# Where GpSimd's record scatters stand in layer 0 of a graph network: in one run ahead of the row gathers, or in four parts between later stages

## The chip, the cores and the metric

The kernel runs on one core of a Trainium2 chip. The metric is the device time of one execution in microseconds; a time "of the kernel" is the median of several executions. Profiled executions are single ones and have a time of their own.

## The reference, cut to what matters

Four layers work on 3125 nodes of 256 features and on 53125 edges (50000 random ones and a loop at every node). Each layer adds a sum over edges and a mixer over nodes, and then a mixture of experts:

```
x = x + _L0_gnn_ref(xn, src, dst, edge_weight, ...) + _L0_mix_ref(xn[None], ...)[0]
x = x + _L0_ffn_ref(_layernorm(x, axis=-1)[None], ...)[0]
```

In layer 0, `_L0_gnn_ref` is `h = xn @ W.T + b`, then `segment_sum(edge_weight * h[dst], src)` and an ELU. `_L0_mix_ref` is linear attention over all nodes (sums of keys times values come first, then each node's query is applied to them), a layer norm, a two-layer network of width 1024 and another layer norm. `_L0_ffn_ref` sends each node through one shared hidden layer of width 1024 and one of eight output layers, the one with the greatest gate. Layers 1 to 3 use other graph sums and mixers; what matters here is that layer 0 sums over edges in order of their source, and that layer 1 (and 2) need the edges in order of their destination.

## The kernel before, in words

**Nodes.** The 3125 nodes stand as 25 tiles of 128 rows, the 25 tiles of x stay in on-chip memory. A "pair" below is two such tiles: the mixer and its two-layer network work on 12 pairs and a single last tile.

**Edges are sorted on the chip.** The class `Sorted` computes for each of the 53125 edges (416 columns of 128) its place in a list that is ordered by one key and padded so that each of 440 blocks ("slots") of 128 edges belongs to one node tile. `put_records` (L193) then moves the edges there: 416 indirect DMAs, issued one after the other by GpSimd, each of which writes 128 records of 16 bytes to scattered rows of a DRAM table. This is done twice: `rec_src` (ordered by source, for layer 0's sum) and `rec_dst` (ordered by destination, for layers 1 and 2). `read` (L358) loads a finished table back, and `tiles_as_columns` (L205, L206) transposes it on TensorE into columns of keys, indices and weights that later instructions use. The two sets of places are computed by `places` (L270 to L282); the second set is put away in DRAM by `leave` and fetched again by `take` (the loads of `posi` and `r` from `kept_dst`), because the space is needed in between.

**Layer 0's graph sum.** `project` (L422) writes h to DRAM. `weighted_sums` goes over the 440 slots: `gather` (L503), an indirect DMA issued by GpSimd, fetches the 128 rows of h that the slot's edges name, VectorE builds a selection matrix (L540), TensorE multiplies the two (`aggp`, L542), and VectorE adds the product to the slot's node tile in `acc` (L544). Six tiles `g` take turns as targets of the gathers.

**The mixer is interleaved by a generator.** `mix0` is a generator of 140 steps. The caller takes `ahead` of them before the graph sum (1000 before the change, which means all of them), and the sum takes one step after every second slot while there are steps left. Its normalising step transposes node tiles (`pt`, L460, copied by ScalarE at L462); then come keys and values (`kvp`), and for each pair queries, attention, the two-layer network (`hp`, `fp`, all through L422, with ScalarE's activation at L1048) and `y` (L1054).

**Who decides the order.** The kernel is written in a tile framework: a scheduler puts each engine's instructions into one order from the program's order, the dependences and its own estimate of when things are ready, and a pool's tile is handed out again when its last reader is done. The engines run their own lists in order and wait for one another by semaphores. GpSimd's list is what this change is about. Before the change it reads: the iota `itile` (L275) of the first sort, 416 `rec_src`, `itile` of the second sort, the zeroing of `acc`, then 416 `rec_dst` mixed with the first 79 gathers, the other gathers, 25 row scatters `f0xs`, 25 row gathers `yrow`, then layer 1's gathers `gk`.

**The expert stage.** `ffn0` normalises x, computes the hidden layer and the gate for 7 groups of up to 4 tiles ("the dense part" below), and the places of the nodes in order of expert; `put_rows` (L1424) scatters the 25 node tiles to `f0xs` in DRAM; `all_biases` (L1318 to L1323) adds the gated bias for 25 tiles; then 8 groups of 4 tiles are loaded back (`x4`, L1557), transposed, sent through the hidden layer and their expert (`yp`, L1568) and stored to `f0ys` (L1571); `take_rows` (L1450) gathers the results into node order (`yrow`). `list_by_dst` reads the `rec_dst` table back, transposes it and stores three rows of it for layer 1.

Of the kernel before, what the change touches and what calls it, by code (L numbers as in the profile page):

```python
# [26 lines left out]
ET = 416  # L27
# [4 lines left out]
NB = NT + 1  # L32
SL = 440
BIG = 1e30
GROUPS = [list(range(t, min(t + 4, NT))) for t in range(0, NT, 4)]
PAIRS = [list(range(t, min(t + 2, NT))) for t in range(0, NT, 2)]

# [66 lines left out]
def edges(c):  # L104

    nc, cp = c.nc, c.const

    c.part = cp.tile([P, 1], F32, name="part")
    nc.gpsimd.iota(c.part, pattern=[[0, 1]], base=0, channel_multiplier=1, allow_small_or_imprecise_dtypes=True)
    c.iota = cp.tile([P, P], F32, name="iota")  # L110
    nc.gpsimd.iota(c.iota, pattern=[[1, P]], base=0, channel_multiplier=0, allow_small_or_imprecise_dtypes=True)
    in_order(c)
    c.by_src = Sorted(c, "src", c.w, ("dst", "edge_weight"), (0, 0))
    c.weights = cp.tile([P, SL], F32, name="weights")
    c.by_src.scatter()
    c.by_dst = Sorted(c, "dst", c.ordered, ("src", "edge_type_64", "dst"), (NP, 0, -1))
    c.by_dst.leave()


# [66 lines left out]
    return v.rearrange("p t -> (p t)").rearrange("(r q e) -> r q e", q=4, e=P)  # L186


def put_records(c, rec, r, at, name):

    nc, tc = c.nc, c.tc
    for t in range(ET):
        i = nc.gpsimd.indirect_dma_start(out=rec, in_=r[:, t, :], in_offset=None,  # L193
                                         out_offset=bass.IndirectOffsetOnAxis(ap=at[:, t:t + 1], axis=0))
        if t:
            tc.declare_no_dep(i.ins, group=f"places {name}", reason="their rows are apart")
        tc.add_to_no_dep_group(f"places {name}", i.ins)


def tiles_as_columns(c, wp, pp, src, dst, n):  # L200

    d = dst.rearrange("p (r q) -> p r q", q=4)
    for q in range(4):
        ps = pp.tile([P, n], F32, name="tcp", tag="tcp")
        c.nc.tensor.transpose(ps, src[:, q, :], c.ident[:n, :n])  # L205
        c.nc.vector.tensor_copy(d[:, :, q], ps)  # L206


def places(c, wp, pp, blk, name, nb=NB):
# [78 lines left out]
class Sorted:  # L288
# [58 lines left out]
        nc.sync.dma_start(self.r.rearrange("p t d -> p (t d)"), self.kept[:, :4 * ET])  # L347
        nc.sync.dma_start(self.at.bitcast(F32), self.kept[:, 4 * ET:])

    def scatter(self):  # L350
        put_records(self.c, self.rec, self.r, self.at, self.key)

    def read(self, more=None):


        c, m = self.c, SL // 4
        b = self.rp.tile([m, 4, P, 4], F32, name="back", tag="r")
        c.nc.sync.dma_start(b, self.rec[:SL * P].rearrange("(r q e) d -> r q e d", q=4, e=P))  # L358
        with c.tc.tile_pool(name="bkp", bufs=2, space=PSUM) as pp:
            for k, d in enumerate((self.k, self.i, more)):  # L360
                if d is not None:
                    tiles_as_columns(c, None, pp, b[:, :, :, k], d, m)
        return b

    def close(self):
# [3 lines left out]
def list_by_dst(c):  # L369

    nc, s = c.nc, c.by_dst
    s.scatter()
    b = s.read()
    c.keys, c.types = (c.dram.tile([SL * P], F32, name=k) for k in ("keys", "types"))
    c.ends = c.dram.tile([SL * P + 2], F32, name="ends")
    nc.sync.dma_start(c.ends[:1], c.low[:1, 0])
    nc.sync.dma_start(c.ends[SL * P + 1:], c.low[:1, 0])
    for j, d in ((0, c.keys), (2, c.types), (3, c.ends[1:SL * P + 1])):
        k = s.rp.tile([SL // 4, 4, P], F32, name=f"row{j}")
        nc.vector.tensor_copy(k, b[:, :, :, j])  # L380
        nc.sync.dma_start(d.rearrange("(r q e) -> r q e", q=4, e=P), k)
    s.close()
# [117 lines left out]


def gather(c, dst, table, idx, t):
    c.nc.gpsimd.indirect_dma_start(out=dst, out_offset=None, in_=table,  # L503
                                   in_offset=bass.IndirectOffsetOnAxis(ap=idx[:, t:t + 1], axis=0))


def nodes(table, t0, n):
# [19 lines left out]
def weighted_sums(c, wp, pp, table, beside):  # L527

    nc = c.nc
    s = c.by_src  # L530
    acc = wp.tile([P, NT, D], F32, name="acc", bufs=1)
    nc.gpsimd.memset(acc, 0.0)  # L532
    for t0 in range(0, SL, 8):
        at = blocks_at(c, s, t0, mybir.EngineType.DVE)
        for j in range(8):
            t = t0 + j
            g = wp.tile([P, D], F32, name="g", bufs=6)
            gather(c, g, table, s.i, t)
            sel = wp.tile([P, P], F32, name="sel", bufs=4)
            nc.vector.tensor_scalar(sel, c.iota, s.k[:, t:t + 1], c.weights[:, t:t + 1], op0=ALU.is_equal, op1=ALU.mult)  # L540
            ps = pp.tile([P, D], F32, name="aggp", tag="agg")
            nc.tensor.matmul(ps, sel, g, start=True, stop=True)  # L542
            a = acc[:, bass.ds(at[j], 1), :]
            nc.vector.tensor_add(a, a, ps[:, None, :])  # L544
            if t % 2:
                next(beside, None)
    for _ in beside:
        pass
    return acc


def gnn0(c, wp, pp, xT, beside, ahead):
    nc = c.nc
    table = c.dram.tile([NROW, D], F32, name="h0")
    project(c, wp, pp, xT, load(c, wp, "L0_gnn_W"), table, load_rows(c, wp, "L0_gnn_b"), bufs=1)
    for _ in zip(beside, range(ahead)):
        pass
    acc = weighted_sums(c, wp, pp, table, beside)

    def finish():  # L560
        for t0 in range(0, NT, 5):
            a = acc[:, t0:t0 + 5, :]
            m = wp.tile([P, 5, D], F32, name="elu", tag="proj", bufs=1)
            nc.vector.tensor_scalar_min(m, a, 0.0)
            nc.scalar.activation(m, m, AF.Exp)
            nc.vector.scalar_tensor_tensor(a, a, 0.0, m, op0=ALU.max, op1=ALU.add)
            xs = c.x[:, t0:t0 + 5, :]
            nc.vector.scalar_tensor_tensor(xs, a, -1.0, xs, op0=ALU.add, op1=ALU.add)

    return finish  # L570


def gnn3(c, wp, pp, xT, beside, ahead):
    table = c.dram.tile([NROW, D], F32, name="h3")
    project(c, wp, pp, xT, load(c, wp, "L3_gnn_weight"), table)
    for _ in zip(beside, range(ahead)):
        pass
    acc = weighted_sums(c, wp, pp, table, beside)

    def finish():  # L580
        for t0 in range(0, NT, 5):
            xs = c.x[:, t0:t0 + 5, :]
            c.nc.vector.scalar_tensor_tensor(xs, acc[:, t0:t0 + 5, :], 0.0, xs, op0=ALU.max, op1=ALU.add)

    return finish
# [834 lines left out]
def put_rows(c, table, places, rows, name):  # L1420

    for pl in places:
        for t in range(NT):
            i = c.nc.gpsimd.indirect_dma_start(out=table, out_offset=bass.IndirectOffsetOnAxis(ap=pl[:, t:t + 1], axis=0),  # L1424
                                               in_=rows[:, t, :], in_offset=None)
            c.tc.declare_no_dep(i.ins, group=name, reason="their rows are apart")
            c.tc.add_to_no_dep_group(name, i.ins)


def experts_of(c, te, t0, n, engines):  # L1430
# [11 lines left out]
def take_rows(c, wp, table, places, weights):  # L1442

    nc = c.nc
    for t in range(NT):
        for pl, w in zip(places, weights):
            y = wp.tile([P, D], F32, name="yrow", bufs=6)
            gather(c, y, table, pl, t)
            x = c.x[:, t, :]
            nc.vector.scalar_tensor_tensor(x, y, w[:, t:t + 1], x, op0=ALU.mult, op1=ALU.add)  # L1450

# [63 lines left out]
def ffn0(c):  # L1515
# [3 lines left out]
    n = 32  # L1519
    with ExitStack() as s:  # L1520
# [11 lines left out]
        with tc.tile_pool(name="f0a", bufs=2) as xa, tc.tile_pool(name="f0ap", bufs=2, space=PSUM) as pp:  # L1532
            xn = xa.tile([P, NT, D], F32, name="xn", bufs=1)
# [13 lines left out]
            pm = largest(c, wp, p, NT, "pm")  # L1547
            co = first(c, wp, p, pm, NT, "co")
            places, te = token_tiles(c, wp, [co], n)
            put_rows(c, xs, places, xn, "f0")  # L1550
            nc.vector.tensor_mul(co, co, p)
            all_biases(c, wp, pp, co, bd)
        lp = s.enter_context(tc.tile_pool(name="f0l", bufs=2))
# [1 line left out]
        for t0 in range(0, n, 4):  # L1555
# [13 lines left out]
                                     start=f == 0, stop=f == 7)  # L1569
                nc.vector.tensor_copy(y4[:, j, :], ps[:, 0, :])  # L1570
            nc.sync.dma_start(nodes(ys, t0, 4), y4)  # L1571
        take_rows(c, lp, ys, places, [pm])


def ffn1(c):
# [122 lines left out]
def mixed(c, i):  # L1698

    tc = c.tc  # L1700
    with ExitStack() as s:
        lp = s.enter_context(tc.tile_pool(name=f"l{i}", bufs=1))
        xT = lp.tile([P, 2, NP], F32, name="xT")
        norm = normalise(c, xT, mp=lp)
        if i == 0:
            c.by_src.read(c.weights)
        gp = s.enter_context(tc.tile_pool(name=f"g{i}", bufs=2))
        gpp = s.enter_context(tc.tile_pool(name=f"g{i}p", bufs=3 if i == 1 else 2, space=PSUM))
        sums = (gnn0, gnn1, gnn2, gnn3)[i]
# [9 lines left out]
        mpp = s.enter_context(tc.tile_pool(name=f"m{i}p", bufs=2, space=PSUM))  # L1719

        beside = (mix0, mix1, mix2, mix3)[i](c, mp, mpp, xT, norm)
        finish = sums(c, gp, gpp, xT, beside, (1000, 8, 8, 8)[i])
        if finish:
            finish()
        if i == 0:
# [3 lines left out]
@with_exitstack  # L1729
def tile_net(ctx, tc, w, out):  # L1730
    c = Net(ctx, tc, w)
    load_x(c)
    constants(c)
    edges(c)
    for i, experts in enumerate((ffn0, ffn1, ffn2, ffn3)):
        mixed(c, i)
        if i == 0:
            c.by_dst.take()
        experts(c)
        if i == 0:  # L1740
            list_by_dst(c)
    store_x(c, out)
# [65 lines left out]
```

## Time and profile before

| | |
|---|---|
| time, median of 3 runs | 8027.63 us (8026.4 to 8031.22) |
| the profiled execution's own time | 8002.89 us |
| its span, first to last instruction | 8001.1 us |
| its mean granted TensorE clock | 0.718 |
| busy share of the span: TensorE, VectorE, ScalarE, GpSimd | 63%, 41%, 12%, 41% |
| `rec_src` scatters on GpSimd | 416, about 114 to 669 us of the span |
| `rec_dst` scatters on GpSimd | 416, 740.0 to 1478.9 us |
| layer 0's gathers on GpSimd | 440, 920.1 to 2161.6 us |
| `f0xs` row scatters, `yrow` row gathers | 25 and 25, from 2384.5 and from 2676.6 us |

The profile is one execution. Its page gives the busy time of each engine and groups of instructions by line; the trace behind it gives each instruction with its start, duration and the time its engine sat idle before it, with the event that ended that idle time ("remote" and "issue" mean that none of the recorded events fits). Times along the span are in microseconds from its start. The profiled execution is 24.7 us, or 0.31%, shorter than the median of the timed runs.

### The profile page before, as it was taken

What the parts mean: (1) busy time and instruction counts of PE and PEld (TensorE: products, weight loads), DVE (VectorE), ACT (ScalarE), POOL (GpSimd) and SP (SyncE); (2) the same over time, 40 slices, a digit from 0 to 9 for tenths busy, and PEclk for the clock granted to TensorE, in tenths of its full rate; (3) what the DMA queues carried; (4) which work ended last, traced back from release to release, by engine and by line L of the source; (5) the groups of instructions that cost most, each with busy time, mean ns of one, the idle gap of its engine ahead of it and who ended that gap; (6) DMA issues with size and microseconds to landing.
All of it is one profiled execution on the core that took longest, in us unless ns stands there. A gap on an engine that the chain in (4) does not pass through costs nothing. (4 is left out here: it accounts for less than half of the span.)

```text
span 8001.1 us, 59679 instructions
## 1 busy us (share of the span) xinstructions
PE 5059.4 (63%) x16612; PEld 3257.6 (41%) x16612; DVE 3313.0 (41%) x8158; ACT 966.9 (12%) x2062; POOL 3283.8 (41%) x3301
## 2 busy tenths in 40 slices
PE   5102323577599776775655795765555998877755
PEld 1001212354265455553333453543433555555334
DVE  3002211354510357766557335544444112545443
ACT  0000001221022111100000011100001223222011
POOL 3775665545500155555762204334341000444632
PEclk6556656787678876666666697865557999988558
DMA  5000100122311244442333113222222000212333
GB/s 170 3 2 20 24 17 16 43 62 75 80 51 43 75 120 128 131 133 75 91 90 86 70 52 108 76 77 78 76 75 60 0 0 30 70 56 62 92 88 110
DMA packets 290607, 542.97 MB, mean 68 GB/s; under 512 B 79731, under 2 KB 170801, under 8 KB 288221
## 3 DMA queue, kind: packets, MB, share of 16 engines
q0 software_dynamic: 144224, 324.84, 15.0%
q1 hardware_dynamic: 146057, 214.25, 8.2%
q8 instruction: 148, 2.42, 0.1%
q14 instruction: 178, 1.46, 0.1%
HBM read 457.51 MB, written 81.97 MB: 67 GB/s over the span
## 5 line engine op out<-in xcount | busy, mean ns | idle before, releaser
L503 POOL DMA_INDIRECT g<-h,si_src x880 | 848.2, 964 | 895.5 <-PE aggp L542 581.3
L542 PE MATMUL aggp<-g,sel 128*128 128x256 f32 x1760 | 717.3, 528 | 361.3 <-DMA g<-h,si_src 155.0
L503 POOL DMA_INDIRECT g<-h,si_dst x440 | 472.6, 1074 | 733.2 <-issue 621.5
L542 PEld LDWEIGHTS aggp<-g,sel 128*128 128x128 f32 x1760 | 368.3, 246 | 659.8 <-issue 338.7
L503 POOL DMA_INDIRECT gk<-tk,si_dst x440 | 431.2, 980 | 448.1 <-DVE sc L751 214.9
L544 DVE TENSOR_TENSOR acc<-acc,aggp 128x256 f32 x880 | 366.8, 417 | 559.3 <-PE aggp L542 250.3
L770 PE MATMUL aggp<-gv,sel 128*128 128x260 f32 x880 | 380.3, 589 | 266.2 <-DVE big L772 134.0
L503 POOL DMA_INDIRECT gv<-tv,si_dst x440 | 445.5, 1013 | 232.8 <-issue 119.3
L909 PE MATMUL aggp<-g,sel 128*128 128x264 f32 x880 | 412.8, 609 | 183.4 <-issue 124.1
L193 POOL DMA_INDIRECT rec_src<-r,posi x416 | 428.2, 1029 | 205.6 <-issue 127.1
L193 POOL DMA_INDIRECT rec_dst<-r,posi x416 | 404.9, 973 | 137.1 <-issue 126.2
L748 PE MATMUL qxp<-big,keyT 128*128 x880 | 335.5, 540 | 192.8 <-DVE keyT L600 154.9
L770 PEld LDWEIGHTS aggp<-gv,sel 128*128 128x128 f32 x880 | 224.7, 283 | 421.5 <-DVE big L772 181.8
L422 PE MATMUL hp<-yT,w_L_mix_W 128*128 128x256 f32 (+1 forms) x624 | 198.6, 470 | 216.4 <-issue 154.9
L909 PEld LDWEIGHTS aggp<-g,sel 128*128 128x128 f32 x880 | 218.3, 290 | 272.6 <-issue 133.8
L888 PE MATMUL trgp<-own,keyT 128*128 x880 | 183.4, 339 | 226.1 <-DVE z L892 225.7
L748 PEld LDWEIGHTS qxp<-big,keyT 128*128 128x128 f32 x880 | 221.2, 265 | 254.2 <-issue 179.5
L532 POOL MEMSET acc<- 128x6400 f32 x2 | 10.9, 5432 | 760.3 <-ACT xT L462 706.0
L540 DVE TENSOR_SCALAR sel<-iota,sk_src,weights 128x128 f32<-128x128 f32 x880 | 299.3, 364 | 0.0
L888 PEld LDWEIGHTS trgp<-own,keyT 128*128 128x128 f32 x880 | 188.9, 310 | 263.7 <-DVE z L892 249.7
L422 PE MATMUL hp<-xT,w_L_ffn_W 128*128 128x512 f32 (+1 forms) x672 | 293.1, 581 | 0.2
L1327 DVE SCALAR_TENSOR_TENSOR x<-yp,lg,x 128x256 f32<-128x256 f32 x200 | 94.2, 484 | 443.2 <-PE yp L422 443.1
(514 smaller groups left out, 9043.3 us busy)
## 6 DMA issues: line engine op xcount, KB each, us to landing
keyT<-keys SPq DMA_DIRECT2D x110, 256.0 KB
keyT<-keys SPq DMA_DIRECT2D x55, 512.0 KB
g<-h,si_src POOLq DMA_INDIRECT x880
typeT<-types SPq DMA_DIRECT2D x110, 128.0 KB
w_L_ffn_Wd<-in_L_ffn_Wd SPq DMA_DIRECT2D x8, 1024.0 KB
w_L_ffn_W<-in_L_ffn_W SPq DMA_DIRECT2D x16, 512.0 KB
f1xs<-zero SPq DMA_DIRECT2D x1, 7424.0 KB
f3xs<-zero SPq DMA_DIRECT2D x1, 7424.0 KB
```

The lines of the kernel that those rows point to most:

```text
L193: i = nc.gpsimd.indirect_dma_start(out=rec, in_=r[:, t, :], in_offset=None, out_offset=bass.IndirectOffsetOnAxis(ap=at[:, t:t + 1], axis=0))
L422: c.nc.tensor.matmul(out, a, b, start=k == 0, stop=k == last)
L503: c.nc.gpsimd.indirect_dma_start(out=dst, out_offset=None, in_=table, in_offset=bass.IndirectOffsetOnAxis(ap=idx[:, t:t + 1], axis=0))
L532: nc.gpsimd.memset(acc, 0.0)
L540: nc.vector.tensor_scalar(sel, c.iota, s.k[:, t:t + 1], c.weights[:, t:t + 1], op0=ALU.is_equal, op1=ALU.mult)
L542: nc.tensor.matmul(ps, sel, g, start=True, stop=True)
L544: nc.vector.tensor_add(a, a, ps[:, None, :])
L748: nc.tensor.matmul(qx[:, j:j + 1, :], selT[:, (i + j) * P:(i + j + 1) * P], q[:, bass.ds(at[t0 % 8 + i + j], 1), :], start=True, stop=True)
L770: nc.tensor.matmul(ps, sel[:, j, :], g[:, j, :], start=True, stop=True)
L888: nc.tensor.matmul(px[:, j:j + 1, :], selT[:, j * P:(j + 1) * P], own[:, bass.ds(at[j], 1), :], start=True, stop=True)
L909: nc.tensor.matmul(ps, sel[:, j, :], g[:, j, :], start=True, stop=True)
L1327: c.nc.vector.scalar_tensor_tensor(x, y, coef[:, e:e + 1], x, op0=ALU.mult, op1=ALU.add)
```

## The change

The order of GpSimd's instructions in layer 0 is written out. `behind(c)` asks the scheduler to issue what is inside it after the last scatter or gather recorded in `c.last`; it sets the order of issue only and adds no wait for data. The 416 `rec_dst` scatters are cut at `SPLIT`: 24 stand behind the `rec_src` scatters, 150 behind the last layer-0 gather, 190 behind the `f0xs` row scatters and 52 in `list_by_dst`, and `take_rows`'s gathers stand behind those. The reading of `rec_src` moves from ahead of the graph sum's pools to a point behind the first 95 of the mixer's 140 steps, with its transposes and copies pinned to their place in the program.

```diff
+SPLIT = (24, 174, 364)
...
     c.by_dst = Sorted(c, "dst", c.ordered, ("src", "edge_type_64", "dst"), (NP, 0, -1))
+    with behind(c):
+        c.by_dst.scatter(range(SPLIT[0]))
     c.by_dst.leave()
...
+def behind(c):
+    return c.tc.issue_after(c.last)
...
-def put_records(c, rec, r, at, name):
+def put_records(c, rec, r, at, name, tiles=range(ET)):
...
-    for t in range(ET):
+    for t in tiles:
...
+    c.last = i.ins
...
+        a = c.nc.tensor.transpose(ps, src[:, q, :], c.ident[:n, :n])
+        b = c.nc.vector.tensor_copy(d[:, :, q], ps)
+        if pin:
+            pinned(c, a)
+            pinned(c, b)
...
 def list_by_dst(c):
-    s.scatter()
+    with behind(c):
+        s.scatter(range(SPLIT[2], ET))
     b = s.read()
...
-            gather(c, g, table, s.i, t)
+            c.last = gather(c, g, table, s.i, t).ins
...
-def gnn0(c, wp, pp, xT, beside, ahead):
+def gnn0(c, wp, pp, xT, beside, ahead, then=None):
...
     for _ in zip(beside, range(ahead)):
         pass
+    if then:
+        then()
     acc = weighted_sums(c, wp, pp, table, beside)
...
-            put_rows(c, xs, places, xn, "f0")
+            with behind(c):
+                put_rows(c, xs, places, xn, "f0")
+            with behind(c):
+                c.by_dst.scatter(range(SPLIT[1], SPLIT[2]))
...
-        take_rows(c, lp, ys, places, [pm])
+        with behind(c):
+            take_rows(c, lp, ys, places, [pm])
...
-        if i == 0:
-            c.by_src.read(c.weights)
...
-        finish = sums(c, gp, gpp, xT, beside, (1000, 8, 8, 8)[i])
+        finish = sums(c, gp, gpp, xT, beside, (95, 8, 8, 8)[i], *([lambda: c.by_src.read(c.weights)] if i == 0 else []))
...
         if i == 0:
             c.by_dst.take()
+            with behind(c):
+                c.by_dst.scatter(range(SPLIT[0], SPLIT[1]))
         experts(c)
```

More of the change, by code (lines that the diff above doesn't have):

```diff
@@ L186, in by_tiles, with pinned @@
     return v.rearrange("p t -> (p t)").rearrange("(r q e) -> r q e", q=4, e=P)
-def put_records(c, rec, r, at, name):
+def behind(c):
+    return c.tc.issue_after(c.last)
+def pinned(c, i):
+    c.tc.keep_in_program_order(i)
+def put_records(c, rec, r, at, name, tiles=range(ET)):
     nc, tc = c.nc, c.tc
-    for t in range(ET):
+    for t in tiles:
         i = nc.gpsimd.indirect_dma_start(out=rec, in_=r[:, t, :], in_offset=None,
@@ L197, in put_records, with tiles_as_columns @@
         tc.add_to_no_dep_group(f"places {name}", i.ins)
-def tiles_as_columns(c, wp, pp, src, dst, n):
+    c.last = i.ins
+def tiles_as_columns(c, wp, pp, src, dst, n, pin=False):
     d = dst.rearrange("p (r q) -> p r q", q=4)
@@ L204, in tiles_as_columns @@
         ps = pp.tile([P, n], F32, name="tcp", tag="tcp")
-        c.nc.tensor.transpose(ps, src[:, q, :], c.ident[:n, :n])
-        c.nc.vector.tensor_copy(d[:, :, q], ps)
+        a = c.nc.tensor.transpose(ps, src[:, q, :], c.ident[:n, :n])
[3 more added lines that the diff above has]
+            pinned(c, b)
 def places(c, wp, pp, blk, name, nb=NB):
@@ L348, in take, with scatter @@
         nc.sync.dma_start(self.at.bitcast(F32), self.kept[:, 4 * ET:])
-    def scatter(self):
-        put_records(self.c, self.rec, self.r, self.at, self.key)
+    def scatter(self, tiles=range(ET)):
+        put_records(self.c, self.rec, self.r, self.at, self.key, tiles)
     def read(self, more=None):
@@ L361, in read @@
                 if d is not None:
-                    tiles_as_columns(c, None, pp, b[:, :, :, k], d, m)
+                    tiles_as_columns(c, None, pp, b[:, :, :, k], d, m, pin=True)
         return b
@@ L502, in gather @@
 def gather(c, dst, table, idx, t):
-    c.nc.gpsimd.indirect_dma_start(out=dst, out_offset=None, in_=table,
-                                   in_offset=bass.IndirectOffsetOnAxis(ap=idx[:, t:t + 1], axis=0))
+    return c.nc.gpsimd.indirect_dma_start(out=dst, out_offset=None, in_=table,
+                                          in_offset=bass.IndirectOffsetOnAxis(ap=idx[:, t:t + 1], axis=0))
 def nodes(table, t0, n):
@@ L570, in gnn0, with gnn3 @@
     return finish
-def gnn3(c, wp, pp, xT, beside, ahead):
+def gnn3(c, wp, pp, xT, beside, ahead, then=None):
     table = c.dram.tile([NROW, D], F32, name="h3")
@@ L577, in gnn3 @@
         pass
+    if then:
+        then()
     acc = weighted_sums(c, wp, pp, table, beside)
@@ L1427, in put_rows @@
             c.tc.add_to_no_dep_group(name, i.ins)
+    c.last = i.ins
 def experts_of(c, te, t0, n, engines):
@@ L1447, in take_rows @@
             y = wp.tile([P, D], F32, name="yrow", bufs=6)
-            gather(c, y, table, pl, t)
+            i = gather(c, y, table, pl, t)
             x = c.x[:, t, :]
```

## The prediction

> **What bounds the kernel now.** I read the slices of the page first (part 2: 40 slices of 200 us).
>
> ```profile
> PE   5102323577599776775655795765555998877755
> ...
> POOL 3775665545500155555762204334341000444632
> ```
>
> From 0 to 1400 us TensorE is busy 0 to 5 tenths while GpSimd is busy 5 to 7, so layer 0 is not bound by arithmetic there. The tile view of the scatters says what GpSimd does.
>
> ```profile
> L193 POOL DMA_INDIRECT rec_dst<-r,posi x416: 954/958/1482, 740.0 to 1478.9; - x139
> ```
>
> One scatter takes 0.96 us, and the gap to the next is 0.30: 1.265 us each (the gathers: 0.95 + 0.30). 416 scatters fill 526 us of the 739, and 79 gathers 99. Next the windows, by stage: PE, PEld, DVE, ACT, POOL busy with their instruction counts, TensorE's granted clock, DMA share, GB/s.
>
> ```profile
> 165.00:341.00 176.00, 43.69 (x60) 11.88 (x59) 12.58 (x21) 0.00 (x0) 133.62 (x140) 0.50 0.03 2
> 785.00:890.00 105.00, 18.89 (x36) 10.77 (x36) 4.65 (x13) 0.83 (x2) 77.21 (x81) 0.53 0.05 8
> ...
> 1513.00:1874.00 361.00, 282.91 (x1086) 210.57 (x1085) 192.61 (x614) 108.99 (x191) 155.20 (x157) 0.87 0.19 57
> 1913.00:2161.00 248.00, 160.40 (x346) 77.76 (x344) 116.56 (x344) 0.00 (x0) 165.03 (x175) 0.64 0.33 91
> 2198.00:2384.00 186.00, 173.70 (x687) 115.28 (x688) 23.26 (x84) 50.50 (x92) 0.00 (x0) 0.78 0.13 51
> 2417.00:2677.00 260.00, 248.05 (x863) 159.53 (x863) 19.62 (x49) 58.09 (x105) 0.43 (x1) 0.95 0.10 33
> 7740.00:7770.00 30.00, 5.82 (x12) 2.04 (x12) 1.68 (x4) 0.76 (x3) 22.69 (x25) 0.50 0.29 104
> ```
>
> The striking rows are the first two and the last. GpSimd issues scatters back to back, and TensorE gets through 119 instructions (matmuls and weight loads) in 176 us, 72 in 105, 24 in 30: one per 1.48, 1.46 and 1.25 us. In the gather stage (1513 to 1874) it is one per 0.17. No engine is near full in the slow rows. VectorE's timeline in layer 3's bias loop shows the onset.
>
> ```profile
> 7730.81 0.42 DVE L1323 TENSOR_TENSOR x<-x,cbp 128x256 f32<-128x256 f32 x1 [1.50 <-PE cbp L1322]
> ...
> 7760.35 0.42 DVE L1323 TENSOR_TENSOR x<-x,cbp 128x256 f32<-128x256 f32 x1 [7.98 <-remote]
> ```
>
> The loop and its data are the same; after some 18 of 50 row scatters in a row the wait rises from 1.50 to 7.98 us, with nothing named. ScalarE in `ffn0`'s bias loop goes from 1.67 to 6.06 beside the 25 `f0xs`, and is back at 1.67 some 5 us after the last of them. So a train of scatters slows hand-overs from TensorE to about 1.4 us per instruction, after its first 20 or so. The place of the scatters matters more than their 1.265 us.
>
> A page speaks against this reading. The Trainium skill, "SBUF — State Buffer", section "Who interferes with whom", says that only the port pair shared by VectorE and GpSimd causes contention, that TensorE and ScalarE wait on nobody, and that DMA does not contend with engines. ScalarE's 6.06 us for a copy out of TensorE's result disagrees with it; by the page the sum would be that of the first rival.
>
> **Part 1, up to the last gather.** The order on GpSimd changes to: `itile`, 416 `rec_src`, `itile`, 24 `rec_dst`, `acc`, 440 gathers, 150 `rec_dst`, 25 `f0xs`, 241 `rec_dst`, 25 `yrow`. The iota that the second sort needs still stands behind the 416 `rec_src`:
>
> ```profile
> PE tbp L280 <- DVE itile L276: 349.7, 1, 349.7
> ```
>
> TensorE waits 349.7 us for it, to 677, and normalising follows at 703. TensorE's new order has this wait first too, so steps called "ahead" do not fill that idle time.
> - From 703: normalising, keys/values and projection ran undisturbed at 703–757 and 900–938, 92 us, and I add 11 for the few that got through between: 103. The 24 scatters start at 740 and last 31; I add 10 (0 to 31).
> - Then 8 pairs without gathers. Pairs under scatters end every 145 us (1081, 1231, 1374, 1502); from 1546 to 1901 they take 45.1 with about 19.6 gathers each. Nearest rows: a gather more in a pair added 1.1 us, which leaves 24 at least; the chain of its stages gives 33 to 36, no change 45. I take 35: 280 us. So 1096.
> - 4 pairs with 22 gathers (47.7 each) and the last tile (39): 230 us and 111 gathers; the first gather 5 us after 1096.
> - 329 gathers remain. The tail of before is the row: 165 in 237 us, 1.436 each, 472 us (at the bare 1.25 of GpSimd: 411). Ends at 1803; finishing as before 36 us: 1839.
>
> Before, finishing ended at 2198. Gain 359 us.
>
> **Part 2, 150 scatters beside the dense part.** They start behind the last gather, 1804, and last 190 us, to 1994. The dense part would run 1839 to 2025 (186 us, 1376 TensorE instructions in the trace). By 1839 28 scatters are out, so it begins slow: 155 us at 1.4 are 111 instructions, 15 us of its work; from 1994 the other 171 follow: `f0xs` at 2165 instead of 2025.5. Loss 139.5 (0 to 3 if nothing slows: the scatters are then out before `f0xs`).
>
> **Part 3, 25 `f0xs` and 241 scatters.** 266 × 1.265 = 336 us, from 2165 to 2501. Before, `f0xs` to `yrow` took 292 us: 25 bias tiles (6 instructions each) and 8 expert groups (224 each). Some 12 bias tiles pass before the slowing, 13 take 8.4 us each, which ends 132 us in; the other 204 us give 146 instructions of group 1, 19 us of its 29. What is left at 2501 is 259 − 19 less the 22 us of loading ahead, 218, and some 4 for the end of the slowing: `yrow` at 558 us after `f0xs`, a loss of 266. There is also a new wait. On SyncE the load of `back` stands behind the sixth `x4` load and waits for all 416 records; on VectorE the copy of `back` stands among the `y` copies of expert group 4; behind it are the y copies of groups 4 to 8, and TensorE, which lacks free result tiles. With nothing slowed this alone gives 336 + 8 for the load + 126 for the rest = 470, so +178. That is the lower bound of this part; under the slowing it is covered.
>
> **Part 4.** Transposes and copies of `rec_dst` behind the expert loop, and the `wqkv` load behind the pool that they hold: 3 to 6 us, 4.5 taken. `take`'s two loads on SyncE go behind the stores of h, beside hundreds of us of idle queue: 0. The pinned transposes of `rec_src` (12, with copies) sit inside the mixer: 5, counted.
>
> **Sum.** −359 + 139.5 + 266 + 4.5 = +51: 8053.9 for an execution like the profiled 8002.89. The median lies 24.7 above that: 8079.
>
> **The rivals.**
> - *Nothing slows beside the later scatters (faster).* −359 + 3 + 178 + 4.5 = −173, 7854. For it: those stretches of `ffn0` were never beside 100 scatters, and the dense part streams 8 matmuls per hand-over. Against: the mixer's `hp` streams as much, and ScalarE's `hT` waited 10.7 us each at 1193 to 1214 beside `rec_dst`. It decides from below 0.2 us per instruction.
> - *Only one of the two stages slows.* Only part 3: −359 + 3 + 266 + 4.5 = −86, 7942. Only part 2: −359 + 139.5 + 178 + 4.5 = −37, 7991.
> - *The gain is smaller.* Pairs keep 45 us and the 24 scatters cost 31: +101 on the forecast, 8180. The other way, gathers at 1.25: −61, 8018.
> - *The change does not do what it says.* If the scheduler's order put mixer steps beside `rec_src`, from 342 on, some 330 us more would go. The first wait above speaks against it.
>
> **How the numbers follow.** A measurement of this kernel tells about 0.2% (16 us) from no change. The forecast, with both stages slow, has 0.62; its own range is 8018 (fast gathers) to 8160 (four fifths of the way to the smaller gain). Both stages free 0.16, one of them 0.16, the smaller gain up to 8180 0.06. The forecast's lower end crosses no change in a tenth of the cases, so faster 0.16 + 0.16 + 0.03, same 0.07, slower the rest. The range runs from the rival with one free stage, widened by the gathers' bound (7942 − 61 = 7880), to the forecast's upper end.
>
> **What would show it.** Right: the mixer's first eight pairs 33 to 36 us apart from about 816; the last gather near 1804; TensorE instructions in the dense part 1.2 to 1.5 us apart until 150 scatters are out; `f0xs` near 2165, `yrow` near 2723. Wrong: dense groups at their 26 us beside the scatters, hand-overs in the bias loop at 1.67 us far behind the first 20, or the pairs at 45 us and more without gathers. The first alone takes back 139, and with the second the kernel is faster.

## The result: slower by 1.7%

| | before | changed |
|---|---|---|
| time, median of 4 runs | 8027.01 us (8008.05 to 8031.22) | 8160.97 us (8141.78 to 8172.16) |
| ratio | 1 | 1.0169 (1.0143 to 1.0195) |
| profiled execution, span | 8002.89, 8001.1 us | 8141.78, 8140.0 us |

The profile after, first by slices (TensorE and GpSimd, 40 slices of 203.5 us):

```profile
PE   4204667662723786675666495775554999877656
...
POOL 3773015667174125555664202444342000444632
```

(Each digit is the busy share of one slice in tenths.) The hole in TensorE's row has moved from the fourth to seventh slice to the tenth, twelfth and thirteenth. GpSimd has nothing to do in the fifth slice, where the mixer's first pairs run without it. The tile view of the scatters and the windows of the changed kernel (columns as in the prediction: PE, PEld, DVE, ACT, POOL busy, granted clock, DMA share, GB/s):

```profile
L206 POOL DMA_INDIRECT rec_dst<-r,posi x416: 954/958/2037, 669.6 to 2565.6; - x139
```

```profile
669.00:703.00 34.00, 1.83 (x2) 0.50 (x2) 8.41 (x35) 0.00 (x0) 26.23 (x25) 0.50 0.13 28
860.00:1149.00 289.00, 179.78 (x679) 139.54 (x679) 91.11 (x262) 95.03 (x166) 0.00 (x0) 0.73 0.00 0
1149.00:1394.00 245.00, 188.50 (x684) 131.29 (x684) 130.60 (x416) 63.27 (x113) 119.96 (x121) 0.84 0.22 69
1394.00:1856.00 462.00, 290.34 (x640) 140.85 (x640) 218.89 (x646) 0.16 (x1) 304.70 (x324) 0.67 0.32 91
1856.00:1888.00 32.00, 4.21 (x8) 1.50 (x6) 25.36 (x56) 6.35 (x5) 25.90 (x21) 0.50 0.11 10
1888.00:2052.00 164.00, 39.62 (x101) 23.97 (x101) 13.62 (x46) 11.73 (x20) 123.63 (x129) 0.54 0.18 60
2052.00:2221.00 169.00, 146.65 (x586) 99.22 (x587) 12.88 (x48) 39.22 (x72) 0.00 (x0) 0.76 0.00 1
2254.00:2567.00 313.00, 66.47 (x139) 32.88 (x138) 4.65 (x11) 11.43 (x24) 239.56 (x240) 0.57 0.04 7
2567.00:2804.00 237.00, 203.42 (x720) 133.28 (x720) 14.36 (x33) 46.93 (x81) 0.00 (x0) 0.93 0.12 36
```

Read the sixth and seventh rows together: beside 129 records the dense part got through 202 TensorE instructions (matmuls and weight loads) in 164 us (one per 0.81), without them through 1173 in 169 (one per 0.14). The 164 us are not all slow: until 1911 TensorE started 52 instructions at its own pace, and from 1911 to 2051 it started 149, one per 0.94, with long stretches of exactly one per 1.40. The fifth row fits this: while VectorE did 56 instructions, GpSimd issued only 21 DMAs in 32 us, one per 1.52. The eighth row is the expert stage beside 240 records: 277 instructions in 313 us. VectorE's timeline there shows what that looks like from its side:

```profile
2498.13 0.42 DVE L1596 COPY y<-yp 128x256 f32<-128x256 f32 x1 [171.78 <-remote]
2542.93 0.42 DVE L1596 COPY y<-yp 128x256 f32<-128x256 f32 x1 [44.37 <-remote]
2586.33 0.42 DVE L1596 COPY y<-yp 128x256 f32<-128x256 f32 x1 [42.98 <-remote]
...
2613.68 0.42 DVE L1596 COPY y<-yp 128x256 f32<-128x256 f32 x1 [19.14 <-PE yp L1594]
2617.13 0.42 DVE L1596 COPY y<-yp 128x256 f32<-128x256 f32 x1 [3.03 <-PE yp L1594]
```

Two copies of the same loop are 45 us apart while records are issued and 3.45 us apart 50 us after the last record (which ends at 2566.5). One of the 150 records meant to stand behind the last gather went out among the gathers, at 1160; 149 stand behind it.

| landmark, us from the span's start | before | predicted | after |
|---|---|---|---|
| mixer's normalising starts | 702.8 | 713 | 731.0 |
| eighth pair done | 1675.9 | 1096 | 1146.1 |
| last gather issued | 2160.4 | 1803 | 1853.0 |
| dense part's first `hp` on TensorE | 2205.4 | 1846 | 1898.5 |
| `f0xs` | 2384.5 | 2165 | 2221.4 |
| `yrow` | 2676.6 | 2723 | 2804.7 |
| layer 1's first `gk` | 2806.4 | 2857 | 2936.3 |

### The profile page after: what moved, and what is told of

Read it like the earlier page. It is cut to its first block, busy times and chain, and to the rows that moved or that the text cites. A ratio compares the mean times of both kernels' runs of the same rounds, so it can differ in the third digit from the quotient of the medians.

```text
span 8140.0 us, 59766 instructions
## 1 busy us (share of the span) xinstructions
PE 5064.8 (62%) x16612; PEld 3248.8 (40%) x16612; DVE 3331.4 (41%) x8158; ACT 966.6 (12%) x2060; POOL 3285.1 (40%) x3301
## 5 line engine op out<-in xcount | busy, mean ns | idle before, releaser
L934 DVE TENSOR_TENSOR acc<-acc,aggp 128x264 f32 x385 | 164.1, 426 | 190.1 <-PE aggp L931 185.9
```

## The experiments

Theory A, from the prediction: GpSimd's scatters in a train (many in a row, each as soon as the one before is issued) slow every TensorE instruction to 1.25 to 1.5 us. The rivals are named with each run. The runs took place on several chips, and this turned out to matter: the chips of runs 1 to 4 and 13 to 18 and of the result above take 8027 to 8044 us for the kernel before (called first kind below), those of runs 5 to 12 take 7535 to 7542 (second kind). Whether it is the chip itself or something else that differed between these sets of runs, none of them separates.

**Run 1, the disputed cost by itself.** The network is replaced by phases such as

```diff
+    for k in range(60):
+        ps = pp.tile([P, P], F32, name="lp")
+        c.nc.tensor.matmul(ps, c.ident, s, start=True, stop=True)
+        s = c.wp.tile([P, P], F32, name="ls", bufs=2)
+        c.nc.scalar.copy(s, ps)
```

beside which GpSimd issues its train. In the trace, one such matmul is two weight loads and two matmuls. The eleven phases run one after the other.

> This kernel leaves the whole network out and stores x. It runs eleven phases with a barrier ahead of each: a chain of 60 steps of one matmul and one ScalarE copy of its result, alone and beside 100 record scatters (128 x 16 bytes), 100 gathers (128 x 256 bytes) into separate places, 100 memsets of GpSimd, 40 scatters with a long memset behind each, 60 with a short memset behind each, and 6 bursts of 10 with long memsets between them; 20 groups of 8 accumulating matmuls and one copy, alone and beside 100 scatters; 60 steps of ScalarE and VectorE without TensorE, alone and beside 100 scatters. Theory A (a train of scatters slows each TensorE instruction to 1.25 to 1.5 us): beside the 100 scatters, after some 20 of them, a step of the chain takes 2.5 to 3 us (one weight load, one matmul) and a group of 16 instructions 20 to 24 us; the chain without TensorE is unchanged; memsets change nothing. Theory B (each hand-over between engines is delayed by some 8 us, however many instructions it has): both chains take about 8 us a step and the group of 8 matmuls also 8 more. Theory C (any indirect DMA issued at this rate does it, gathers too): the gathers' phase is as slow as the scatters'. If the train matters and not the single scatter, the phases with memsets between and with bursts of 10 keep the pace of the chain alone.

Alone a step took 1.15 us. Beside 100 scatters it stayed at 1.15 for 18 steps (22 us) and then rose to 5.60, to return to 1.15 some 14 us after the last scatter. ScalarE's timeline of three phases: beside scatters, beside gathers, and beside scatters with a memset of 128 x 300 between.

```profile
140.25 0.27 ACT L1760 COPY ls<-lp 128x128 f32<-128x128 f32 x1 [5.33 <-remote]
145.85 0.27 ACT L1760 COPY ls<-lp 128x128 f32<-128x128 f32 x1 [5.33 <-issue]
...
305.87 0.27 ACT L1760 COPY ls<-lp 128x128 f32<-128x128 f32 x1 [5.33 <-remote]
311.47 0.27 ACT L1760 COPY ls<-lp 128x128 f32<-128x128 f32 x1 [5.33 <-remote]
...
660.63 0.27 ACT L1760 COPY ls<-lp 128x128 f32<-128x128 f32 x1 [0.89 <-PE lp L1758]
661.78 0.27 ACT L1760 COPY ls<-lp 128x128 f32<-128x128 f32 x1 [0.89 <-PE lp L1758]
```

5.60 for four TensorE instructions is 1.40 each, and a group of 8 accumulating matmuls (32 instructions) took 44.8 and 44.1 us, again 1.40 each. Theory B (per hand-over) is out. Theory C holds: gathers do it as well, when nothing makes them wait. A chain of ScalarE and VectorE alone went from 0.59 to 1.4 us a step too, some 32 us into its train, which theory A did not expect: the slowing is not TensorE's own. VectorE's side of that chain, before and after the onset:

```profile
1111.65 0.23 DVE L1779 COPY lv<-ls 128x128 f32<-128x128 f32 x1 [0.36 <-ACT ls L1777]
...
1116.46 0.23 DVE L1779 COPY lv<-ls 128x128 f32<-128x128 f32 x1 [1.17 <-ACT ls L1777]
```

GpSimd's memsets alone changed nothing. Nor did 40 scatters with a long memset behind each, or 60 in runs of 6 to 10 with memsets between (the order in which the scheduler put that phase). With a short memset behind each scatter (one per 1.50 us instead of 1.265) the chain kept its 1.15 throughout.

**Run 2, the later records left out.**

```diff
     for t in tiles:
+        if name == "dst" and t >= SPLIT[0]:
+            break
```

> The changed kernel without the last 392 of the 416 dst records, so layers 1 and 2 sum over other edges; layer 0 is whole. Theory A (the scatters slow all that TensorE does beside them): layer 0 up to the last gather stays as in the changed kernel, near 1855; the dense part takes 186 us instead of 333 and f0xs to yrow 292 instead of 583, together 438 less: yrow near 2366 instead of 2804. Rival (the longer dense part and expert stage come from the new order of the other instructions, or from a lower clock): the two stages keep more than half of their extra 438 us.

The same two stages without records:

```profile
1892.00:2071.00 179.00, 171.41 (x680) 113.76 (x680) 18.05 (x63) 47.85 (x88) 0.00 (x0) 0.80 0.10 42
2103.00:2364.00 261.00, 247.74 (x860) 158.91 (x860) 17.37 (x41) 58.14 (x106) 0.20 (x2) 0.95 0.11 33
```

Last gather 1849.1, the dense part 179 us from its first `hp` to `f0xs`, `f0xs` to `yrow` 292.1, `yrow` at 2363.8: the expected 2366 within 3 us. The two stages lose all their extra time with the records, so it is the records and not the order of the rest. The granted clock, 0.54 and 0.57 beside records, is 0.80 and 0.95 here. A lower clock does not explain the slow stretch of the dense part: from 1989 to 2040 a `lgp` matmul there lasts 0.17 us, and the next starts 2.80 us later. The total, 8064.4 us, is not comparable, since layers 1 and 2 gather other rows.

**Run 3, no records beside the dense part.**

```diff
-SPLIT = (24, 174, 364)
+SPLIT = (24, 25, 364)
```

> The changed kernel with SPLIT (24, 25, 364): one record instead of 150 behind the last gather, and 390 instead of 241 behind f0xs. Theory A: the dense part is back at 186 (147 less), and the longer train behind f0xs adds 149 x 1.265 = 188, so about 41 us more than the changed kernel, 8200. Rival (the dense part hides a share of its records, because its matmuls stream and hand over seldom): the dense part was no dearer than its records, so moving them costs the whole 188: 8300 or more; if part 3 hides the records in the bias loop, up to 147 less, 8015.

8194.01 us, ratio 1.0207 (1.0175 to 1.0239); 8200 was expected. The dense part is back at 179 us, `f0xs` to `yrow` is 769 (583 + 188 = 771). On this kind of chip a record costs nearly its own 1.265 us wherever it stands beside TensorE's work: the 120 that ran beside the changed kernel's dense part cost it 144 us (323 less 179), 1.20 each, and the 149 moved behind `f0xs` 186, 1.25 each. Little of them is hidden.

**Run 4, gathers earlier beside the mixer.**

```diff
-        finish = sums(c, gp, gpp, xT, beside, (95, 8, 8, 8)[i], *([lambda: c.by_src.read(c.weights)] if i == 0 else []))
+        finish = sums(c, gp, gpp, xT, beside, (30, 8, 8, 8)[i], *([lambda: c.by_src.read(c.weights)] if i == 0 else []))
```

> The changed kernel with 30 mixer steps instead of 95 ahead of the gathers, so that 254 instead of 113 gathers are issued beside the mixer's pairs and 176 instead of 317 behind them. In the changed kernel pairs without gathers took 41.1 us and pairs with 22 gathers 48.6, and a gather behind the mixer 1.43. Theory (gathers are nearly free beside pairs): 8 pairs take 7.5 us more each, 60, and 141 gathers fewer in the tail save 202: 142 less, 8019. Rival (GpSimd's gathers beside the pairs cost their own 1.25 us each there too): no gain, 8150 to 8170.

7987.68 us, ratio 0.9939 (0.9917 to 0.9961): 173 less than the changed kernel (142 was expected) and 0.6% below the kernel before. Its windows, beside the pairs and behind them:

```profile
857.00:1381.00 524.00, 407.04 (x1522) 296.06 (x1521) 274.24 (x874) 150.82 (x263) 232.33 (x234) 0.86 0.21 61
1418.00:1679.00 261.00, 188.23 (x366) 87.88 (x365) 125.87 (x373) 1.58 (x2) 172.83 (x183) 0.58 0.33 91
```

11 pairs beside 234 gathers took 47.6 us each, against 41.5 without any; a gather behind the mixer costs 1.44. Gathers are nearly free beside pairs, and the 95 steps ahead of them gave that away.

**Runs 5 to 8, pacing, on a chip of the second kind.** Pacing here means a short memset of GpSimd's behind each scatter, so that the train is issued more slowly. The edit of run 5, with the same in the loop of `put_rows`:

```diff
+def pause(c, n, ins):
+    with c.tc.issue_after(ins):
+        return c.nc.gpsimd.memset(c.pause[:, :n], 0.0).ins
...
+        with (c.tc.issue_after(p) if p else ExitStack()):
+            i = nc.gpsimd.indirect_dma_start(out=rec, in_=r[:, t, :], in_offset=None,
+                                             out_offset=bass.IndirectOffsetOnAxis(ap=at[:, t:t + 1], axis=0))
...
+        p = pause(c, 300, i.ins) if name == "dst" else None
```

> The changed kernel with a memset of 128 x 300 on GpSimd behind each dst record scatter and each of the expert stages' row scatters, kept in this order. In the phases of the first run a scatter with such a memset took 1.50 us instead of 1.265, and the chain on TensorE kept its 1.15 us a step instead of 5.6. Theory A (a train that is faster than about 1.4 us per scatter is what slows the engines): the mixer starts near 703 instead of 731; the dense part takes 186 us but f0xs waits for 150 x 1.5 = 225 us of records, so it starts about 225 us behind the last gather instead of 365; records end 25 x 1.5 + 241 x 1.5 = 399 us later, then 8 for the load and 126 for the rest of the expert groups: yrow some 533 us behind f0xs instead of 583. Together about 218 less: 7943. Rival (the number of scatters in flight counts, or their mere presence): nothing is sped up and the memsets add 416 x 0.235 = 98 us: 8260.

Run 6 adds run 4's edit:

> The fifth run's memsets together with the fourth run's 30 steps ahead. If the two gains are independent: 7988 - 218 = 7770. Rival (they are the same gain, since both only fill GpSimd's idle time): 7940 or more.

Run 7 paces the src records too and exchanges two lines, which brings the second `itile` ahead of the src records on GpSimd:

```diff
-    c.by_src.scatter()
     c.by_dst = Sorted(c, "dst", c.ordered, ("src", "edge_type_64", "dst"), (NP, 0, -1))
+    c.by_src.scatter()
```

> The changed kernel with the memsets behind every record and row scatter, the src ones too, and with the src scatters traced behind the second sort, so that the iota which the second sort needs stands ahead of them. Theory A: the second sort is not slowed (pos every 2.3 us instead of 8.4), TensorE's wait of 300 to 350 us for the iota is gone, the mixer starts between 215 and 300 and its 95 steps end near 670 to 750; src records end at 114 + 416 x 1.5 = 738, the 24 dst ones at 774; 111 gathers beside 4 pairs and one tile in 240 us, 329 in 470: last gather near 1485 instead of 1855. With the later stages as in the fifth run: 8161 - 370 - 190 = 7600. Rival (the mixer beside the src records is slowed as the pairs beside unpaced dst records were): the last gather not before 1750, total 7860 or more.

> As the first run, without the network, other phases: the chain of matmul and copy beside 100 scatters with a memset of 16, of 100 and of 200 columns behind each; beside 100 scatters of 64 rows instead of 128 and no memset; 80 copies of ScalarE that wait for nobody, beside 100 scatters; 80 of VectorE; 80 steps of ScalarE and VectorE in turn; and 100 scatters with nothing beside them. Theory A1 (there is a limit of about 1.4 us per scatter of 128 rows, GpSimd alone issues at 1.265, and what is too much builds up): the phase with 16 columns is slowed at some point, later than without; 200 columns (about 1.45 us) not; 64 rows not; independent copies drop to one per 1.4 us on each engine, which makes it the issue of instructions and not the hand-over. Rival A2 (any wait of GpSimd's between scatters is enough): 16 columns already leave the chain at 1.15. Rival A3 (only hand-overs are slowed): the independent copies keep their pace.

Runs 5, 6 and 7 took 7484.51, 7322.70 and 7194.43 us beside 7541.59: ratios 0.9922 (0.9905 to 0.9938), 0.9700 and 0.9534. These do not test pacing, for this chip slows nothing. In run 5 the src records are not paced, and yet the second sort's steps beside them are 2.1 us apart; every phase of run 8 kept the chain's 1.15, and 80 steps of ScalarE and VectorE kept 0.63 beside an unpaced train.

**Run 9, the changed kernel on another chip of the second kind.**

> The changed kernel itself, beside the kernel before on the same chip. The fifth to eighth runs took place on another chip than the first four: the kernel before took 7541 us there instead of 8030, and its trains of scatters without memsets slowed nothing (the second sort's steps 2.1 us apart instead of 8.4, in the fifth run). Theory A (the slowing belongs to some chips, and the prediction's price of the later trains is that of such a chip): on a chip without it the changed kernel is faster than before, by the prediction's first rival 173 us plus or minus 50, 7320 to 7420 beside 7541; on a chip with it 8160 beside 8030 again. Rival (the waits of the new order cost as much without any slowing): slower than before on either chip.

7440.13 us beside 7534.84: ratio 0.9872 (0.9855 to 0.9888), 95 us less. The sign of the change goes with the kind of chip. Its windows (dense part, expert stage with records, expert stage after them) and VectorE's timeline at the records' end:

```profile
1728.00:1906.00 178.00, 170.44 (x680) 112.38 (x678) 17.87 (x64) 47.44 (x86) 116.18 (x121) 0.81 0.13 43
1938.00:2242.00 304.00, 141.35 (x472) 87.25 (x472) 8.05 (x19) 36.90 (x66) 230.91 (x241) 0.72 0.09 18
2242.00:2362.00 120.00, 104.02 (x376) 71.32 (x376) 9.13 (x21) 20.22 (x35) 0.86 (x2) 0.93 0.15 44
```

```profile
2060.66 0.42 DVE L1596 COPY y<-yp 128x256 f32<-128x256 f32 x1 [3.03 <-PE yp L1594]
2251.05 0.62 DVE L398 COPY row<-back 110x512 f32<-110x512 f32 x1 [189.96 <-DMA back<-rec_dst]
2251.58 0.42 DVE L1596 COPY y<-yp 128x256 f32<-128x256 f32 x1
```

The dense part takes its 178 us beside 121 records. Four expert groups run through, then VectorE stands 190 us at the copy of `back` until all records are out: the new wait of the prediction's part 3, bare. `f0xs` to `yrow` is 455 (470 was its price without slowing). The gathers behind the mixer take 1.25 us each here, 1.44 on the first kind.

**Runs 10 to 12, on the chip of run 9.**

> The fifth run's kernel again. On a chip where trains slow the engines, theory A: 218 less than the changed kernel, 7943 beside 8030. On one where they do not: 0.235 us a record of pure cost where GpSimd is waited for, so 50 to 100 more than the changed kernel, and the same 7485 as before.

> The seventh run's kernel again. On a chip where trains slow the engines: if pacing avoids it all, the same stages as in the seventh run up to the last gather (near 1397) and a total some 560 to 620 below the changed kernel, near 7570; if pacing avoids only a part, between 7600 and 7900. On a chip without it: 7195 as before.

> The eighth run's phases, with a first one added (100 scatters without memsets beside the chain) and longer trains of independent copies. On a chip where trains slow the engines: the first phase goes to 5.6 us a step; with 16 columns (1.27 us per scatter) slowed, with 200 (1.42) not, with 100 (1.33) between; 64 rows not; independent copies of ScalarE and VectorE one per 1.4 us after some 22 us if the issue of instructions is what is slowed, unchanged if only hand-overs are. On a chip without: every phase at its own pace, the first one too.

Runs 10 and 11 took 7471.92 (0.9921) and 7172.82 us (0.9524), and no phase of run 12 left its pace. Without slowing, pacing is a cost: 32 us against run 9.

**Runs 13 to 15, on a chip of the first kind.** Run 13 is the kernel before.

> The kernel before, for its profile on this call's chip. On a chip where trains of scatters slow nothing: the second sort's steps 2.1 us apart, pairs beside the dst records about 45 to 60 us instead of 145, the gathers' tail 1.25 us each, yrow near 2270 (the changed kernel's 2362 there less what its total gained, 95, the other way round: near 2455). On a chip with the slowing: the profile of before.

> The memsets behind the dst records and row scatters. On a chip where trains slow the engines, theory A (a scatter every 1.5 us is below what builds up): about 218 less than the changed kernel, ratio to before near 0.99. Rival (pacing helps the small chain of the first run only): ratio 1.017 to 1.03. On a chip without: 0.992 again.

> Memsets behind all scatters and the iota ahead of the src records. On a chip where trains slow the engines, theory A: 7570 beside 8030, ratio 0.94; rival: over 0.97. On a chip without: 0.953 again.

Run 13 took 8048.92 us, with pairs beside records 129 to 147 us apart, as on the chip of the prediction's profile. Run 14: 7893.67 us beside 8037.15, ratio 0.9825 (0.9801 to 0.9849); run 15: 7555.47 us, 0.9402 (0.9380 to 0.9425). Run 14's dense part and its expert stage up to the last record, then the mixer's first eight pairs in run 15 (GpSimd's counts include the memsets):

```profile
1893.00:2074.00 181.00, 173.04 (x682) 114.40 (x682) 23.65 (x68) 47.60 (x87) 160.85 (x243) 0.79 0.13 43
2111.00:2471.00 360.00, 199.74 (x700) 129.08 (x700) 10.61 (x25) 49.55 (x86) 319.90 (x483) 0.77 0.09 21
```

```profile
217.00:643.00 426.00, 295.53 (x1118) 214.93 (x1118) 162.66 (x439) 127.07 (x241) 379.05 (x562) 0.78 0.05 11
```

On the kind of chip where the changed kernel lost 134 us, the same order with one memset per scatter wins 143. A ratio of 0.99 was expected. The dense part runs in 181 us with some 120 scatters beside it (323 us in the changed kernel), and `f0xs` to `yrow` falls from 583 to 451 us; there the wait at the copy of `back` shows (182.83 us). 533 was expected for it: only 54 us of expert work stood behind the last record, where 134 had been allowed. In run 15 the mixer's start and its first eight pairs run beside src records, from 217 to 643, 41.6 us a pair, where before TensorE waited for the iota.

**Runs 16 to 18, on the same chip.** Run 16 is run 15 with 130 steps ahead instead of 95.

> The fifteenth run's kernel with 130 instead of 95 mixer steps ahead of the gathers. There 8 pairs were done at 643 and TensorE then had nothing until the src records were read at 790. Theory: nearly all pairs are done by 643 + 4 x 41 = 807, the 440 gathers then run alone, at 1.43 us each on a chip with the slowing (788 + 629 = 1417 instead of 1491) and 1.25 on one without (1337 instead of 1392): 55 to 75 us less than the fifteenth run's kernel, ratio to before 0.932 or 0.945. Rival (the gathers alone take longer than beside pairs, since they are bound by their consumers): no gain, 0.940 or 0.953.

7494.78 us beside 8043.86: ratio 0.9329 (0.9306 to 0.9353), 61 us below run 15; the best version tried. Twelve pairs are done at 813 and the last gather is at 1447.5 (1417 expected: 1.45 us each).

> The twelfth run's kernel again. On a chip where trains slow the engines: first phase 5.6 us a step; 16 columns (1.27 us per scatter) slowed; 200 columns (1.42) not; 100 (1.33) tells where the limit lies; 64 rows without memset not; independent copies of ScalarE and VectorE one per 1.4 us after some 22 us if the issue of instructions is slowed, unchanged if only hand-overs are. On a chip without: every phase at its own pace.

| train beside the chain | us per scatter, first 20 | chain, us a step |
|---|---|---|
| no memset | 1.27 | 5.60 after 18 steps |
| memset of 16 columns | 1.29 | up to 4.9, then 2.1 to 3.5, after 16 |
| memset of 100 columns | 1.34 | 2.1 to 4.9, then 2.8, after 22 |
| memset of 200 columns | 1.41 | 1.15 throughout |
| 64 rows, no memset | 1.21 | 5.60 after 10 |

So the limit lies between one indirect DMA per 1.34 us and one per 1.41, and it goes by the DMA instruction and not by its rows, as far as 64 and 128 rows tell. In the phases with 16 and 100 columns GpSimd's own pace fell to 1.43 and 1.42 from the 21st scatter on. ScalarE's 250 copies, which wait for nobody, went from one per 0.20 us to this:

```profile
840.68 0.30 ACT L1786 COPY la<-s 128x128 f32<-128x128 f32 x1 [1.11 <-ACT la L1786]
842.07 0.30 ACT L1786 COPY la<-s 128x128 f32<-128x128 f32 x1 [1.09 <-ACT la L1786]
843.48 0.30 ACT L1786 COPY la<-s 128x128 f32<-128x128 f32 x1 [1.11 <-ACT la L1786]
```

Steadily one per 1.40 us, from 820 to 899. Hand-overs are not needed: it is the starting of instructions, on TensorE and ScalarE alike. For VectorE only the chain of run 1 speaks, where its copies wait 1.17 us instead of 0.36. VectorE's 300 copies in run 17 tell nothing on this, since they kept GpSimd from working:

```profile
936.26 0.96 POOL L1802 DMA_INDIRECT t<-r,idx  x1 [28.51 <-SPq L1838]
937.52 39.58 POOL L1802 DMA_INDIRECT t<-r,idx  x1 [0.30 <-issue]
977.41 0.96 POOL L1802 DMA_INDIRECT t<-r,idx  x1 [0.30 <-issue]
```

The Trainium skill, "SBUF — State Buffer", section "Who interferes with whom", says that a VectorE copy in its two-port mode locks GpSimd out for as long as it runs; the second scatter took 39.58 us and ended at 977.10, 0.1 us behind the last of the 300 copies (936.10 to 976.98, back to back), which agrees. That these copies ran in this mode the trace does not say.

> The kernel before, for its profile on this call's chip. On a chip without the slowing: the second sort's steps 2.1 us apart; pairs beside dst records 45 to 75 us instead of 145; gathers' tail 1.25 each; f0xs to yrow near the 292 of before. On one with it: the profile of before.

Run 18, the kernel before on this chip, is 8039.08 us: the profile of before again. No run gave its profile on a chip of the second kind.

## Why the prediction was wrong, by its steps

The direction held and so did the main mechanism, but +134 was measured where +51 was forecast, a microsecond outside the range. Between the two profiled executions the change is +139, a miss of 88 us: 52 in part 1, 4 in part 2, 25 in part 3, −3 in part 4, and 9 in the layers behind, which the forecast held constant (9 us is within the spread of single executions, 8008 to 8031 for the kernel before).

- **Part 1, the step that failed: "I take 35".** Pairs without gathers take 41.5 us each (855.6 to 1146.1, seven steps), 46 us more over these seven steps. The rows offered 24 to 45, and the value was taken from a sum of the stages' durations; the nearest measured row was the pair with gathers, 45.1. Run 4 shows why the slope misled: 21 gathers add only 6 us to a pair, 0.3 each where the prediction took 1.1. The prediction priced this as a rival ("The gain is smaller", pairs at 45 and the 24 scatters at 31: +101); about half of that came. Its "every 145 us" for pairs under scatters is 140 by its own four marks; no term rests on it.
- **Part 1, the 24 records.** The prediction placed them at 740, where the kernel before has its first one. On GpSimd they stand right behind the src records and run from 669.6, just when the second sort ends; in the window 669 to 703 TensorE does 4 instructions and VectorE 35. The mixer starts 28 us later than before; 10 were allowed. From there to the end of the first pair it took 125 us instead of 103 + 35, which gives 13 back; no run shows which of the two terms was too high.
- **Part 1, the rest.** Four pairs and the last tile took 244 us from the end of the eighth pair, against 235 (230, and 5 to the first gather). The gathers left then took 463 against 472, at the forecast 1.44 us each.
- **Part 2** was right in sum, in part by luck: 323 us from the first `hp` to `f0xs`, 319 forecast (179 and 139.5). The slow stretch has its 1.40 us per instruction, but the dense part did not begin slow: TensorE ran at its own pace until 1911, 57 us into the train, which between 1856 and 1888 was issued at one per 1.52 us only. And the pace came back only some 16 us behind the last record (2050.7), where none was allowed. The two cancel. Run 2 confirms the cause and run 14 that the pace of the train is what matters.
- **Part 3** was right in kind and 25 us short: records end 345 us after `f0xs` (336), and `yrow` comes 238 us behind them (222). The forecast allowed 4 us for the end of the slowing; TensorE had its pace again 28 us behind the last record (2566.5 to 2594.6).
- **Part 4**: `yrow` to `gk` took 132 us (130 before).
- **The first rival is real, on other chips.** Run 9 has the dense part at 178 us, `f0xs` to `yrow` at 455 and the bare wait at `back`, as its sum has them. It forecast −173 and −95 came. Which of its terms is short there stays open, as no trace shows the kernel before on such a chip. But its −359 was worked out from a profile in which the kernel before is slowed too (its pairs beside records are 128 to 150 us apart); on a chip that slows nothing that gain has less to come from.
- **The page's rule.** That TensorE and ScalarE wait on nobody does not hold on the first kind of chip, where run 1 has 5.60 us instead of 1.15, and agrees with the phases of runs 8 and 12. Whether the ports that the page speaks of have any part in it, no run shows. The prediction set the row above the rule, and for its chip that was right.

What makes the two kinds of chip differ, which resource sets the limit between 1.34 and 1.41 us, and whether the recording of the profile has a part in it, no run shows.

## What to carry to other kernels

Before moving DMAs into an engine's idle time, look how fast the issuing engine would send them: here one indirect DMA per 1.27 us slowed what TensorE did to a fraction, and one per 1.41 us cost a small chain nothing. In the kernel a filler of 0.36 us behind each (one per 1.50 us) was worth 3.4% (ratio 1.0169 without, 0.9825 with). Where a step is priced between two rows, take the measured row and not the sum of its parts (41.5 came, nearer to the row's 45.1 than to the 35 taken). And a change that trades such trains against waits should be measured on more than one chip: the same edit was 1.7% slower on one and 1.3% faster on another.

## What the runs showed of the hardware that was not expected

- On some chips GpSimd's back-to-back indirect DMAs (scatters of 128 x 16 bytes at 1.265 us, gathers of 128 x 256 bytes at 1.25 us, scatters of 64 rows at 1.20) slow the start of instructions on TensorE and ScalarE to one per 1.40 us. In the small chains this began 12 to 32 us after the train did (within 8 us where TensorE had 32 instructions a step) and ended some 14 us after it; in the kernel it ended 16 and 28 us after the last record. At 1.41 us per DMA the chain was not slowed. In a chain of ScalarE and VectorE each step of two instructions takes 1.4.
- On two other chips none of this was seen: a gather behind the mixer costs 1.25 instead of 1.44 us, and the kernel before takes 7535 to 7542 instead of 8027 to 8044 us.
